# Weights of the first layer ahead of the rows, weight copies on ScalarE, and exactness looks moved between layers, in a graph network on one Trainium2 core

## The chip, the core and the metric

The kernel runs on one core of a Trainium2 chip. The core has a matrix engine (TensorE, PE in the profile; its weight loads are listed apart as PEld), a vector engine (VectorE, DVE), an activation engine (ScalarE, ACT), GpSimd (POOL) and SyncE (SP), which here only issues transfers. SP, ACT and POOL each have their own queue of DMA issues. Each engine works through its own instructions in order; semaphores order them between engines.

The metric is device time in microseconds (us), the median of several runs of one launch.

## The reference

Sixteen graphs of 1024 nodes with 128 features, each with a 1024 by 1024 matrix `adj` of zeros and ones. Two blocks of four layers. The first is a gated network, each graph for itself; the second normalizes over all graphs after each layer. Cut to what matters:

```python
# block 0: h = relu(layernorm(x)), then for i in range(4):
hw = einsum('bnc,cd->bnd', h, weight[i])
m = einsum('bjn,bjd->bnd', adj, hw)
h = gru_cell(m, h, w_ih[i], w_hh[i], b_ih[i], b_hh[i])
x = x + h * mask
# gru_cell: gx = m @ w_ih.T + b_ih; gh = h @ w_hh.T + b_hh
#   r = sigmoid(xr + hr); z = sigmoid(xz + hz); n = tanh(xn + r * hn)
#   h = (1 - z) * n + z * h

# block 1: h = relu(layernorm(x)), then for i in range(4):
h = relu(einsum('bnm,bmc->bnc', adj, h @ W[i]) + b[i])
h = gamma[i] * (h - mean) * rsqrt(var + EPS) + beta[i]   # mean, var over graphs and nodes
x = x + h
```

## The kernel before

The work is in `exact_path`. The features are split into a high part that `fp32r` holds exactly and a low rest; an aggregation with `adj` is a sum of matmuls of both parts with the rows of `adj`. This holds as long as the rows have nothing in their low 16 bits. VectorE looks at each row once for that (`look`, L585 to L589: a maximum over the low halves, 128x1024), and a flag at the end would start a general path, which these inputs don't need.

**Block 0, two streams.** Graphs run in pairs: stream A (`sa`) has the even graphs, stream B (`sb`) the odd ones. `half_step(one, two)` (L823) makes the gates of stream `two` (its matmuls need only h and m) and the aggregation of stream `one`, so that the elementwise work of one hides behind the matmuls of the other. A layer of one graph is: turn h and split it in high (`hw[0]`, ScalarE) and low (`hw[1]`, VectorE), L498 to L503; aggregate with eight rows, 32 matmuls of 512 columns into banks m0 and m1 (L525); copy m from the banks (L750, ScalarE); gates of two halves with six pairs of matmuls each (L762) into four banks g_r, g_hn, g_xn, g_z; sigmoid and tanh on ScalarE (L772 to L778) and five operations on VectorE (L773 to L782). Each gate bank exists once: the second half's matmuls into g_r wait until the first half's sigmoid has read it.

**Weights.** The product `weight[i] @ w_ih[i].T` is made once for each layer. `load_layer` (L457) loads w_hh and w_ih of a layer on SP. `turn_layer` (L466) turns both and weight[i] on TensorE and copies them from the two `tmp` banks; `join_layer` (L484) multiplies and copies w_mT. `load_small` and `turn_small` do the same for biases, gammas and the mask.

**The next pair.** While layer 2 of a stream follows, `ahead` (L787) takes the sums of the next graph's rows of x (`norm_sums`, VectorE), the root (L613, ScalarE, with its own function table), the reciprocal (L617, VectorE) and eight normalizing blocks (L622, ScalarE). `look_on` (L807) makes the looks of a stream's rows: until 3 are done at layer 1, 6 at layer 2 and 8 at layer 3. At layer 1 it also copies and turns the rows for block 1 by GpSimd and SP.

**Order.** For the start (L847 to L952) the order of all five engines is the order of the program, and it is written out by hand: x of graph 0, the rows of `adj` of graphs 0 and 1 (staged as f32, cast by GpSimd or ScalarE in `first_round`), 50 idle transposes for TensorE, norm, split, first aggregation. Weights and looks lie between. After that, only GpSimd and SP keep the program's order; the order of TensorE, VectorE and ScalarE is found by a scheduler when the kernel is built, so that an edit of the looks can move other engines' instructions too.

**Block 1** (L976 to L1149) loads the turned rows again, widens them and aggregates, with the norm over all graphs between layers; then x is added and stored.

Of the kernel before, what the change touches and what calls it, by code (L numbers as in the profile page):

```python
# [8 lines left out]
F32 = mybir.dt.float32  # L9
# [4 lines left out]
AF = mybir.ActivationFunctionType  # L14
ALU = mybir.AluOpType
AX = mybir.AxisListType
P = 128
# [324 lines left out]
def exact_path(  # L342
# [89 lines left out]
    def load_small(prep):  # L432

        vn = prep.tile([P, C], F32, tag="vn", name="vn", bufs=1)[:NV, :]
        r0 = 0
        for src in (g_b_ih, g_b_hh):
            nc.scalar.dma_start(vn[r0 : r0 + 3 * L, :], src.rearrange("l (g c) -> (l g) c", c=C))
            r0 += 3 * L
        for src in (c_b, c_gamma, c_beta):
            nc.scalar.dma_start(vn[r0 : r0 + L, :], src)  # L440
            r0 += L
        mn = prep.tile([P, P], F32, tag="mn", name="mn", bufs=1)
        nc.scalar.dma_start(mn, nodemask.rearrange("b (k p) -> (b k) p", p=P))
        return vn, mn

    def turn_small(vn, mn):
# [19 lines left out]
    def turn_layer(prep, w_g, i):  # L466

        pt = tmp(f"pt_whh{i}")
        for g in range(3):
            nc.tensor.transpose(pt[:, g * P : (g + 1) * P], wns["hh", i][:, g, :], ident)  # L470
        nc.vector.tensor_copy(w_hhT[:, i, :], pt[:, : 3 * P])
        pt = tmp(f"pt_wih{i}")
        for g in range(3):
            nc.tensor.transpose(pt[:, g * P : (g + 1) * P], wns["ih", i][:, g, :], ident)

        w_ihT = prep.tile([P, 3 * C], F32, tag="w_ihT", name=f"w_ihT{i}", bufs=1)
        nc.vector.tensor_copy(w_ihT, pt[:, : 3 * P])
        pg = tmp(f"pt_g{i}")
        nc.tensor.transpose(pg[:, :P], w_g[:, i, :], ident)
        w_gT = prep.tile([P, P], F32, tag="w_gT", name=f"w_gT{i}", bufs=1)  # L480
        nc.vector.tensor_copy(w_gT, pg[:, :P])
        turned[i] = w_gT, w_ihT

    def join_layer(i):  # L484
        w_gT, w_ihT = turned[i]
        pw = tmp(f"pt_wm{i}")
        nc.tensor.matmul(pw[:, : 3 * P], w_gT, w_ihT, start=True, stop=True)
        nc.vector.tensor_copy(w_mT[:, i, :], pw[:, : 3 * P])


    def features_times(w, hT, hw, g, name):
# [42 lines left out]
    with ExitStack() as st:  # L534
# [145 lines left out]
        def behind(*inss):  # L680

            es = ExitStack()
            for ins in () if written[0] else inss:
                es.enter_context(tc.issue_after(ins.ins))
            return es

        class Stream:
# [111 lines left out]
            def finish(self):  # L799

                if self.i == L:
                    self.rest = tail_norm(self.b, self.xt, self.hT)
                    self.b, self.i = self.b + 2, 0
                    if self.b < B:
                        self.take()

            def look_on(self, two):  # L807

                if self.i == 0:
                    return  # L810
                if self.i == 1:
                    if self.b + 2 < B:
                        copy_rows(self.b + 2)
                    adjT = turned_tile(f"adjT{self.b}")
                    for j in range(NB):
                        transpose_rows(self.b, self.rows[j], j, adjT)
                    nc.gpsimd.dma_start(adjT_d[self.b], adjT)
                with behind(two.last_dve):
                    while self.looks < min(3 * self.i, NB):
                        look(self.b, self.rows[self.looks], self.looks)  # L820
                        self.looks += 1

        def half_step(one, two, gated=None, halfway=None):  # L823
# [23 lines left out]
        with tc.tile_pool(name="prep", bufs=1) as prep, tc.manual_schedule(engines=every):  # L847


            pt = tmp("pt_idle")  # L850
            for k in range(50):
                nc.tensor.transpose(pt[:, k % 4 * P : (k % 4 + 1) * P], ident, ident)
            x0 = flat("x0")
            for k0, eng in ((0, nc.sync), (BH, nc.scalar)):
                x0_d = x[0].rearrange("(k p) c -> p k c", p=P)[:, k0 : k0 + BH, :]
                eng.dma_start(x0[:, k0 : k0 + BH, :], x0_d)
            small_in = load_small(prep)
            stage = keep.tile([P, NB, N], BF16, tag="adjT", name="stage", bufs=1).bitcast(F32)
            quarters = [[stage[:, 2 * j : 2 * j + 2, :].rearrange("p a n -> p (a n)")] for j in range(4)]
            late = [[work.tile([P, N], F32, tag="h", name=f"first{j}", bufs=7)] for j in range(4, NB)]  # L860
            raw0 = quarters + late
            first_rows(0, range(4), quarters)
            load_layer(0)
            w_g = flat("w_g")[:, :L, :]
            w_d = g_weight.rearrange("l c d -> c l d")
            nc.sync.dma_start(w_g[:, 0, :], w_d[:, 0, :])
            first_rows(0, range(4, NB), late)
            x1 = load_x(1, nc.sync)
            halves = [[half_tile(f"early{j}_{k}").bitcast(F32) for k in range(2)] for j in range(3)]
            halves.append(  # L870
                [work.tile([P, N], BF16, tag="half1", name=f"early3_{k}", bufs=2).bitcast(F32) for k in range(2)]
            )
            first_rows(1, range(4), halves)
            raw1 = halves + quarters
            h0, h1 = (work.tile([P, N], F32, tag="h", name=f"h_in{b}", bufs=7) for b in range(2))


            sa.open(x0)
            sb.open(x1)
            sa.sums(range(4))  # L880
            norm_root(sa.norm, 0, BH)
            sa.sums(range(4, 5))
            norm_scale(sa.norm, 0, BH)
            sa.sums(range(5, NB))
            sa.normed(range(2))
            norm_root(sa.norm, BH, NB)
            norm_scale(sa.norm, BH, NB)
            sa.normed(range(2, 4))
            sa.split_high(0)
            for j in range(4):  # L890
                sa.rows[j] = first_round(0, j, raw0[j], nc.gpsimd)
            first_look(0, 0, raw0[0])
            sa.split_low(0)
            sa.agg_rows(range(4))
            sa.normed(range(4, NB))
            sa.split_high(1)
            first_look(0, 1, raw0[1])
            sa.split_low(1)
            for j, eng in ((4, nc.scalar), (5, nc.gpsimd)):
                sa.rows[j] = first_round(0, j, raw0[j], eng)  # L900

            turn_small(*small_in)
            turn(sa.y, "in0", h0)
            sa.hT = h0
            first_look(0, 2, raw0[2])
            turn_layer(prep, w_g, 0)
            first_look(0, 3, raw0[3])
            first_rows(1, range(4, NB), quarters)
            sa.agg_rows(range(4, 6))
            join_layer(0)  # L910
            for j, eng in ((6, nc.scalar), (7, nc.gpsimd)):
                sa.rows[j] = first_round(0, j, raw0[j], eng)
            sa.agg_rows(range(6, NB))

            sb.sums(range(NB))
            norm_root(sb.norm, 0, NB)
            norm_scale(sb.norm, 0, NB)
            for j in range(NB):
                sb.rows[j] = first_round(1, j, raw1[j], nc.gpsimd)

            def beside(hf):
                sb.normed(range(hf * BH, (hf + 1) * BH))
                first_look(0, 4 + hf, raw0[4 + hf])

            for hf in range(NH):
                sa.gate_step(hf, lambda: beside(hf))
                sb.split_high(hf)
                sb.split_low(hf)
            for j in (6, 7):
                first_look(0, j, raw0[j])  # L930
            for j in range(4):
                first_look(1, j, raw1[j])
            for i in range(1, L):
                load_layer(i)
            nc.sync.dma_start(w_g[:, 1:, :], w_d[:, 1:, :])
            nc.gpsimd.dma_start(w_c, c_w.rearrange("l c d -> c l d"))
            sb.agg_rows(range(4))
            turn(sb.y, "in1", h1)
            sb.hT = h1
            sb.agg_rows(range(4, NB))  # L940
            sa.ahead()

            def looks():
                for j in range(4, NB):
                    first_look(1, j, raw1[j])

            half_step(sa, sb, looks, lambda: turn_layer(prep, w_g, 1))
            join_layer(1)
            half_step(sb, sa, None, lambda: turn_layer(prep, w_g, 2))
            join_layer(2)  # L950
            turn_layer(prep, w_g, 3)
            join_layer(3)  # L952
# [263 lines left out]
```

## Time and profile before

| | us |
|---|---|
| median of 3 runs | 1866.81 |
| lowest, highest | 1864.57, 1868.89 |
| the profiled execution | 1865.06 |
| its span, first to last instruction | 1863.3 |
| granted TensorE clock, mean | 0.992 |

Busy time of each engine by stage, from the windows view of the profile:

| stage, us | what runs | PE | DVE | ACT | POOL | clock |
|---|---|---|---|---|---|---|
| 0 to 24 | start, first aggregation | 20.46 | 13.55 | 9.43 | 10.02 | 0.93 |
| 24 to 70 | gates and layers 0, 1 of the first pair | 42.14 | 34.70 | 19.44 | 7.91 | 0.96 |
| 70 to 130 | layers 1 to 3 of the first pair | 59.05 | 34.69 | 29.98 | 16.37 | 1.00 |
| 130 to 1233 | the rest of block 0 | 1096.77 | 738.71 | 534.33 | 222.65 | 1.00 |
| 1233 to 1822 | block 1 | 588.65 | 383.00 | 419.85 | 30.71 | 1.00 |
| 1822 to 1863 | last norm, sum, store | 18.73 | 21.94 | 19.33 | 2.62 | 0.74 |

A timeline line has start and duration in us, engine, line of the kernel, operation, what it writes and reads, how many alike are merged (x4), and in brackets the idle time of the engine before it and what ended that. Matmuls overlap, so that the time one takes in the pipeline is longer than the step from one to the next. PEq, ACTq and SPq lines are issues of transfers. Lines of the kernel are given as L and a number.

### The profile page before, as it was taken

What the parts mean: (1) busy time and instruction counts of PE and PEld (TensorE: products, weight loads), DVE (VectorE), ACT (ScalarE), POOL (GpSimd) and SP (SyncE); (2) the same over time, 40 slices, a digit from 0 to 9 for tenths busy, and PEclk for the clock granted to TensorE, in tenths of its full rate; (3) what the DMA queues carried; (4) which work ended last, traced back from release to release, by engine and by line L of the source; (5) the groups of instructions that cost most, each with busy time, mean ns of one, the idle gap of its engine ahead of it and who ended that gap; (6) DMA issues with size and microseconds to landing.
All of it is one profiled execution on the core that took longest, in us unless ns stands there. A gap on an engine that the chain in (4) does not pass through costs nothing. (4 is left out here: it accounts for less than half of the span.)

```text
span 1863.3 us, 21952 instructions
## 1 busy us (share of the span) xinstructions
PE 1825.8 (98%) x7326; PEld 1255.0 (67%) x7326; DVE 1226.6 (66%) x2249; ACT 1032.4 (55%) x1562; POOL 290.3 (16%) x375
## 2 busy tenths in 40 slices
PE   9999999999999999999999999999999999999995
PEld 6556566656656565656665666667778888888884
DVE  7656676666566667667667657676666666666664
ACT  5354453554544445445455453467777768767764
POOL 3042230230131042023023013001100000000021
PEclk9999999999999999999999999999999999999997
DMA  7089776474385376567548546249876666676769
GB/s 253 9 242 300 245 205 226 149 203 165 142 258 181 147 203 192 201 169 223 208 149 203 167 155 175 91 138 333 292 253 227 213 240 222 231 245 209 254 211 258
DMA packets 268433, 381.22 MB, mean 205 GB/s; under 512 B 149812, under 2 KB 171992, under 8 KB 264472
## 3 DMA queue, kind: packets, MB, share of 16 engines
q1 hardware_dynamic: 250112, 245.95, 43.5%
q0 software_dynamic: 17456, 133.45, 20.3%
q8 instruction: 59, 0.97, 0.2%
q14 instruction: 62, 0.51, 0.1%
q10 hardware_dynamic: 744, 0.35, 0.1%
HBM read 287.39 MB, written 117.44 MB: 217 GB/s over the span
## 5 line engine op out<-in xcount | busy, mean ns | idle before, releaser
L525 PE MATMUL pm<-row,ghw 128*128 128x512 f32 x2048 | 520.1, 408 | 2.4 <-ACT ghw L733 1.5
L525 PEld LDWEIGHTS pm<-row,ghw 128*128 128x128 f32 x2048 | 385.0, 189 | 118.8 <-issue 35.9
L525 PE MATMUL pc_m<-wide,chw 128*128 128x512 f32 x1024 | 246.1, 395 | 0.0
L525 PEld LDWEIGHTS pc_m<-wide,chw 128*128 128x128 f32 x1024 | 190.5, 188 | 42.3 <-issue 4.3
L777 ACT ACTIVATE r<-r,vecs 128x512 f32<-128x512 f32 x128 | 92.3, 721 | 215.9 <-DVE r L774 215.8
L525 PE MATMUL pc_g_r<-wide,chw 128*128 128x512 f32 x464 | 187.0, 403 | 0.3 <-ACT chw L502 0.3
L525 PE MATMUL pc_g_z<-wide,chw 128*128 128x512 f32 x464 | 181.0, 390 | 0.0
L594 POOL CAST half<-row 128x1024 bf16<-128x1024 f32 x128 | 140.6, 1114 | 245.9 <-DMA adjT<-half 235.7
L986 DVE CAST wide<-packed 128x1024 fp32r<-128x1024 bf16 x160 | 110.0, 693 | 73.1 <-PE pc_m L525 56.3
L986 DVE CAST wide<-block 128x1024 fp32r<-128x1024 bf16 x160 | 110.2, 691 | 71.9 <-PE pc_g_z L525 36.0
L503 DVE TENSOR_TENSOR ghw<-hw_g,ghw 128x512 fp32r<-128x512 f32 x96 | 62.5, 686 | 121.2 <-ACT ghw L502 121.1
L984 ACT CAST wide<-block 128x1024 fp32r<-128x1024 bf16 x96 | 100.6, 1048 | 60.9 <-PE pc_m L525 34.3
L984 ACT CAST wide<-packed 128x1024 fp32r<-128x1024 bf16 x96 | 100.7, 1049 | 56.5 <-PE pc_g_z L525 27.4
L773 DVE SCALAR_TENSOR_TENSOR r<-g_hn,vecs,r 128x512 f32<-128x512 f32 x128 | 95.3, 744 | 54.4 <-ACT r L772 27.6
L762 PE MATMUL g_xn<-m,w_mT 128*128 128x512 f32 x256 | 130.7, 592 | 0.0
L762 PE MATMUL g_z<-m,w_mT 128*128 128x512 f32 x256 | 130.7, 592 | 0.0
L762 PE MATMUL g_r<-m,w_mT 128*128 128x512 f32 x256 | 130.7, 592 | 0.0
L589 DVE TENSOR_REDUCE low<-row 128x1 f32<-128x1024 uint16 x112 | 130.1, 1204 | 0.0
L750 ACT COPY m<-pm 128x512 f32<-128x512 f32 x128 | 68.6, 587 | 108.6 <-PE pm L525 108.3
L778 ACT ACTIVATE z<-g_z,brz 128x512 f32<-128x512 f32 x128 | 87.2, 681 | 67.7 <-PE g_z L762 67.4
L772 ACT ACTIVATE r<-g_r,brz 128x512 f32<-128x512 f32 x128 | 87.7, 686 | 61.4 <-PE g_r L762 60.3
L1023 DVE BATCH_NORM_STATS2 stats<-feat 128x6 f32<-128x512 f32 x128 | 84.2, 685 | 48.8 <-ACT feat L1022 47.5
(144 smaller groups left out, 2752.9 us busy)
## 6 DMA issues: line engine op xcount, KB each, us to landing
packed<-adjT_d SPq DMA_DIRECT2D x256, 256.0 KB, 6.1
block<-adjT_d SPq DMA_DIRECT2D x256, 256.0 KB, 4.3
raw<-in_adj_dram POOLq DMA_DIRECT2D x112, 512.0 KB, 11.7
row<-raw SPq DMA_DIRECT2D x112, 512.0 KB, 5.4
adjT_d<-adjT POOLq DMA_DIRECT2D x16, 2048.0 KB, 7.8
xmid_d<-x POOLq DMA_DIRECT2D x16, 512.0 KB, 4.6
y<-ymid_d POOLq DMA_DIRECT2D x16, 512.0 KB, 5.2
xo<-xmid_d POOLq DMA_DIRECT2D x32, 256.0 KB, 6.5
```

The costliest lines, as they stand in the source:

```text
L525: nc.tensor.matmul(pm[hf], hw[s][:, j * P : (j + 1) * P], rows[j][:, hf * HALF : (hf + 1) * HALF], start=(j == 0 and s == 0), stop=(j == N ...
L589: nc.vector.tensor_reduce(low[:, k : k + 1], lows, axis=AX.X, op=ALU.max)
L594: nc.gpsimd.tensor_copy(t, row.bitcast(F32))
L750: nc.scalar.copy(m, self.pm[hf])
L762: nc.tensor.matmul(po, wT[:, i, g * C : (g + 1) * C], rhs, start=start, stop=stop)
L772: nc.scalar.activation(r, pr, AF.Sigmoid, bias=brz[:, 3 * i : 3 * i + 1])
L773: nc.vector.scalar_tensor_tensor(r, phn, b_hn(i), r, ALU.add, ALU.mult)
L777: nc.scalar.activation(r, r, AF.Tanh, bias=b_in(i))
L778: self.last_act = nc.scalar.activation(z, pz, AF.Sigmoid, bias=brz[:, 3 * i + 1 : 3 * i + 2])
L984: nc.scalar.copy(r, t)
L986: nc.vector.tensor_copy(r, t)
L1023: nc.vector.bn_stats(stats[:, b * NH + hf, :], dst)
```

## The change

Three edits of the start, and one of the looks.

- The weights of layer 0 (`load_layer(0)` and weight 0) are issued on SP directly behind x's first half, ahead of all rows. Their turn stands ahead of the norm's sums, their join behind the first two normalized blocks. The 50 idle transposes become 20 in front and 30 behind the join. A Sqrt of one column on ScalarE in front of its x transfer loads that table.
- The four copies of `turn_layer` and `join_layer`, for all four layers, go from VectorE to ScalarE.
- The six small transfers go from ScalarE's to GpSimd's queue; in the built order the first of them stands between the two GpSimd instructions that make the identity matrix. `turn_small` moves from ahead of y's turn to behind rows 4 and 5 of the first aggregation.
- `look_on` makes up to four looks at a time, and none when `two` stands at layer 2 with a graph to come, which is when that graph's sums are taken.

```diff
-            nc.scalar.dma_start(vn[r0 : r0 + 3 * L, :], src.rearrange("l (g c) -> (l g) c", c=C))
+            nc.gpsimd.dma_start(vn[r0 : r0 + 3 * L, :], src.rearrange("l (g c) -> (l g) c", c=C))
...
-        nc.vector.tensor_copy(w_hhT[:, i, :], pt[:, : 3 * P])
+        nc.scalar.copy(w_hhT[:, i, :], pt[:, : 3 * P])
...
-        nc.vector.tensor_copy(w_ihT, pt[:, : 3 * P])
+        nc.scalar.copy(w_ihT, pt[:, : 3 * P])
...
-        nc.vector.tensor_copy(w_gT, pg[:, :P])
+        nc.scalar.copy(w_gT, pg[:, :P])
...
-        nc.vector.tensor_copy(w_mT[:, i, :], pw[:, : 3 * P])
+        nc.scalar.copy(w_mT[:, i, :], pw[:, : 3 * P])
...
+                if two.i == 2 and two.b + 2 < B:
+                    return
                 with behind(two.last_dve):
-                    while self.looks < min(3 * self.i, NB):
-                        look(self.b, self.rows[self.looks], self.looks)
+                    for j in range(self.looks, min(self.looks + 4, NB)):
+                        look(self.b, self.rows[j], j)
                         self.looks += 1
...
-            for k in range(50):
-                nc.tensor.transpose(pt[:, k % 4 * P : (k % 4 + 1) * P], ident, ident)
+
+            def idle(n):
+                for k in range(n):
+                    nc.tensor.transpose(pt[:, k % 4 * P : (k % 4 + 1) * P], ident, ident)
+
+            idle(20)
+            root = small.tile([P, 1], F32, tag="root", name="root")
+            nc.scalar.activation(root, eps_t, AF.Sqrt)
...
             small_in = load_small(prep)
+            load_layer(0)
+            w_g = flat("w_g")[:, :L, :]
+            w_d = g_weight.rearrange("l c d -> c l d")
+            nc.sync.dma_start(w_g[:, 0, :], w_d[:, 0, :])
...
-            first_rows(0, range(4), quarters)
-            load_layer(0)
...
-            nc.sync.dma_start(w_g[:, 0, :], w_d[:, 0, :])
-            first_rows(0, range(4, NB), late)
+            first_rows(0, range(NB), raw0)
...
             sb.open(x1)
+            turn_layer(prep, w_g, 0)
             sa.sums(range(4))
...
             sa.normed(range(2))
+            join_layer(0)
+            pt = tmp("pt_idle1")
+            idle(30)
             norm_root(sa.norm, BH, NB)
...
-            turn_small(*small_in)
             turn(sa.y, "in0", h0)
             sa.hT = h0
-            first_look(0, 2, raw0[2])
-            turn_layer(prep, w_g, 0)
-            first_look(0, 3, raw0[3])
+            for j in range(2, 4):
+                first_look(0, j, raw0[j])
             first_rows(1, range(4, NB), quarters)
             sa.agg_rows(range(4, 6))
-            join_layer(0)
+            turn_small(*small_in)
```

More of the change, by code (lines that the diff above doesn't have):

```diff
@@ L436, in load_small @@
         for src in (g_b_ih, g_b_hh):
-            nc.scalar.dma_start(vn[r0 : r0 + 3 * L, :], src.rearrange("l (g c) -> (l g) c", c=C))
+            nc.gpsimd.dma_start(vn[r0 : r0 + 3 * L, :], src.rearrange("l (g c) -> (l g) c", c=C))
             r0 += 3 * L
         for src in (c_b, c_gamma, c_beta):
-            nc.scalar.dma_start(vn[r0 : r0 + L, :], src)
+            nc.gpsimd.dma_start(vn[r0 : r0 + L, :], src)
             r0 += L
         mn = prep.tile([P, P], F32, tag="mn", name="mn", bufs=1)
-        nc.scalar.dma_start(mn, nodemask.rearrange("b (k p) -> (b k) p", p=P))
+        nc.gpsimd.dma_start(mn, nodemask.rearrange("b (k p) -> (b k) p", p=P))
         return vn, mn
@@ L801, in finish @@
                 if self.i == L:
+                    assert self.looks == NB
                     self.rest = tail_norm(self.b, self.xt, self.hT)
@@ L861, in exact_path @@
             raw0 = quarters + late
-            first_rows(0, range(4), quarters)
-            load_layer(0)
-            w_g = flat("w_g")[:, :L, :]
-            w_d = g_weight.rearrange("l c d -> c l d")
-            nc.sync.dma_start(w_g[:, 0, :], w_d[:, 0, :])
-            first_rows(0, range(4, NB), late)
+            first_rows(0, range(NB), raw0)
             x1 = load_x(1, nc.sync)
@@ L898, in exact_path @@
             sa.split_low(1)
-            for j, eng in ((4, nc.scalar), (5, nc.gpsimd)):
-                sa.rows[j] = first_round(0, j, raw0[j], eng)
-            turn_small(*small_in)
+            sa.rows[4] = first_round(0, 4, raw0[4], nc.scalar)
+            sa.rows[5] = first_round(0, 5, raw0[5], nc.gpsimd)
             turn(sa.y, "in0", h0)
             sa.hT = h0
-            first_look(0, 2, raw0[2])
-            turn_layer(prep, w_g, 0)
-            first_look(0, 3, raw0[3])
+            for j in range(2, 4):
+                first_look(0, j, raw0[j])
             first_rows(1, range(4, NB), quarters)
             sa.agg_rows(range(4, 6))
-            join_layer(0)
+            turn_small(*small_in)
             for j, eng in ((6, nc.scalar), (7, nc.gpsimd)):
```

## The prediction

> **What bounds the kernel now.** I read the page first, then busy time by stage, then TensorE's timeline for its idle times, and last the other engines' timelines at each of these.
>
> ```profile
> PE 1825.8 (98%) x7326; PEld 1255.0 (67%) x7326; DVE 1226.6 (66%) x2249; ACT 1032.4 (55%) x1562; POOL 290.3 (16%) x375
> ```
>
> TensorE has work in 98% of the span. Between 1233 and 1822 us it is busy for 588.65 of 589.00 us, and no edit touches that stage or the tail. So the change can win only where TensorE waits, runs at half clock, or does work early that now stands on its path. TensorE's timeline shows these places (start, duration, operation, then the idle time before it and what ended it):
>
> ```profile
> 1.36 7.58 PE L852 MATMUL pt_idle<-ident 128*128 128x128 f32 x50 [1.36 <-POOL ident masks.py:199]
> 10.41 0.70 PE L525 MATMUL pm<-row,ghw 128*128 128x512 f32 x2 [1.47 <-ACT ghw L733]
> 11.42 5.06 PE L525 MATMUL pm<-row,ghw 128*128 128x512 f32 x14 [0.31 <-DVE ghw L737]
> ...
> 62.37 0.33 PE L479 MATMUL pt_g<-ident,w_g 128*128 128x128 f32 x1 [3.10 <-DVE w_hhT L471]
> 62.45 5.50 PE L525 MATMUL pm<-row,ghw 128*128 128x512 f32 x16
> ...
> 93.05 0.91 PE L487 MATMUL pt_wm<-w_ihT,w_gT 128*128 128x384 f32 x2 [0.74 <-DVE w_gT L481]
> ```
>
> Two sets of 16 matmuls take 6.1 and 5.5 us where sixteen take 3.9 at 85.27: the granted clock is 0.71 in 10 to 15 us and 0.83 in 60 to 65. The 3.10 us wait is for a weight copy behind four looks on VectorE:
>
> ```profile
> 57.26 4.59 DVE L589 TENSOR_REDUCE low<-stage 128x1 f32<-128x1024 uint16 x4
> 61.77 0.55 DVE L471 COPY w_hhT<-pt_whh 128x384 f32<-128x384 f32 x1
> ```
>
> In the long stage from 130 to 1233 us TensorE misses 6.2 us in all, in eight waits, of which this is the pattern (VectorE, ScalarE, TensorE):
>
> ```profile
> 239.51 1.18 DVE L589 TENSOR_REDUCE low<-row 128x1 f32<-128x1024 uint16 x1
> ...
> 240.70 2.31 DVE L589 TENSOR_REDUCE low<-row 128x1 f32<-128x1024 uint16 x2
> 242.93 0.19 DVE L617 RECIPROCAL rs_in<-rs_in 128x8 f32<-128x8 f32 x1
> ```
>
> ```profile
> 240.81 0.30 ACT L613 ACTIVATE rs_in<-mv_in,eps_t 128x8 f32<-128x8 f32 x1 [4.31 <-DVE mv_in L610]
> ...
> 243.36 3.18 ACT L622 ACTIVATE y_in<-x,ms_in,rs_in 128x128 f32<-128x128 f32 x8 [0.77 <-DVE ms_in L618]
> ...
> 247.51 1.28 ACT L772 ACT_TABLE_LOAD   x1
> ```
>
> ```profile
> 249.54 1.12 PE L762 MATMUL g_r<-h,w_hhT 128*128 128x512 f32 x2 [0.88 <-ACT r L772]
> ```
>
> Looks delay the last sum and the reciprocal; ScalarE normalizes late, loads the sigmoid's table late, and frees the g_r bank late.
>
> **What the Trainium skill says.** "TensorE: Matmul & The Clock Gate", Part 1: the clock starts at half and is raised after a busy window of about 3.4 us; the windows run freely. The trace agrees: the idle transposes step by 0.213 us until 5.26, then by 0.109; both slow pieces follow a poor window. I use its window below. The same page (Architectural detail) calls ScalarE and VectorE strict FIFO, so an early copy that waits holds everything behind it. "ScalarE: Activation LUTs", What ACT_TABLE_LOAD costs: about 1283 ns a load; here 1.28 us. "DMA: Bandwidth & Descriptors", Queues, rings and completion order: an engine consumes descriptors in ring order; weights put ahead of rows on SP therefore push the rows back. No view isolates that here.
>
> **The change part by part.** The sum is against the profiled execution: 1865.06 us with a span of 1863.3. The median of the three runs is 1866.81, 1.75 above.
>
> *Start, to the first gates (24.00).* Removed from TensorE's path between 16.5 and 24.0: the three turns and the join of layer 0 with their waits. Before, the stretch from the last of the first 16 matmuls (16.41) to the gates takes 7.6 us. What stays: y's turn 0.9, rows 4 and 5 1.9, small vectors 0.5, rows 6 and 7 2.0: 5.3 us.
> Added in front: ident comes 0.9 us later, because a GpSimd DMA now stands between its two parts (such an issue takes 0.89 at 33.00); 20 idle transposes at mostly 0.213 take the engine from 2.25 to about 6.3 (5.9 to 6.5, by where the window falls). The weights (448 KB behind x's first half, sharing the engines with the second, at the 200 to 343 GB/s of the first 10 us, plus 0.6 for landing) are there by about 6.2. Turns to 6.9; ScalarE's three copies 7.0 to 8.3 (0.47 each estimated from 0.587 for 512 columns and 0.39 between 128-column operations); root 8.3 to 8.6 instead of 6.60. The preloaded Sqrt table only makes up for this: before, the root waited for the 1.28 us load. Then scale, two blocks, the join's copy (0.5), second root, two blocks and the high cast: 12.1 instead of 10.27. The join matmul ends at 9.05 and 30 idle transposes at 0.109 end at 12.3. So the first aggregation starts at 12.3, not 10.41; warm, 16 matmuls take 3.7, to 16.1. Rows: some 1.3 us later than before for the first (landed about 7.5, 8.8, 10.1, 11.4), casts on GpSimd 1.04 each, its six issues over by 6.7: not late. The gates start at 21.4: **2.6 us won**. If the window from 5.3 to 8.7, which I put at 70% busy, counts as idle, the 30 transposes run half slow and the start slips 1.5 more: 1.1 won. (45% busy before 12.1 was too little; 78% around 93 was enough.) If the weights land earlier: 3.5.
> This must pass the next chain too: second graph's sums, root, table load, sigmoid (27.71), then VectorE packed from 28.4 to 40.2. Its sums follow the vectors' copies (19.5) and x1's landing (19.95 before, about 18.5 now): sigmoid at 24.7, 3.0 won. So 2.6 holds.
>
> *Layer 1's turn (59 to 68).* ScalarE is idle from 55.7 to 67.8, so the copies follow the turns at once; pt_g starts at 59.5 instead of 62.37 (a bank must still be copied), 2.9 won. No empty window, so no half clock: 16 matmuls in 3.9 instead of 5.5, 1.6 won. The last copy now stands behind two m copies: 0.1 lost. **4.4 won**, 3.5 to 4.8.
>
> *Layers 2 and 3 (83 to 103).* The waits of 0.74 and 0.21 go. But ScalarE now has eight more copies of about 0.5 among eight normalizing blocks (3.2), m copies and two table loads; in the built order w_mT of layer 2 stands behind both m copies, so the gate's m part waits about 1.1. **0**, from 1 won to 1 lost.
>
> *Looks.* Sixteen per pair of graphs as before: A and B each had 3, 3, 2 at layers 1, 2, 3; now A has 4, 0, 4 and B 0, 4, 4. One look is 1.2 us; the additions lie in VectorE's idle times (4.0 us before 300.39, 3.1 before 318.86, against 2.3 more). The built order changes too. At the first place ScalarE now normalizes ahead of the m copies: root 239.65, blocks 240.45 to 243.65, m copies to 244.65, high casts to 245.7, table to 247.0, sigmoid to 247.7. TensorE has moved its m parts behind the h parts, reaches them at 245.0 (the first m copy ends at 244.2), and wants g_r's bank at about 248.1. No wait: six times about 1 us, 5.5 in all, won. At the second (about 268) the build puts 4 instead of 9 matmuls in front of g_r and the blocks ahead of the second m copy: sigmoid ends at 268.4, TensorE arrives at 268.1: 0.35 lost six times, less the 0.63 that two such waits cost today: 1.5 lost. **4.0 won**, 1.5 to 6.
>
> Sum: 2.6 + 4.4 + 0 + 4.0 = 11.0, 1854.1 against the profiled execution, 1855.8 against the median. I take 1855.
>
> **Rivals.** *(a) Head eaten, swaps in the long stage.* The half clock or late weights leave 1 us of the head, layers 2 and 3 lose 1, and the second place takes as much as the first gives: 4.4, 1861. For: idle work now stands in order ahead of real work, and ScalarE is fullest just there (4.53 of 5 us from 90 to 95). Against: 12 us of idle ScalarE at 59 cannot fail to help.
> *(b) All covers hold.* Weights early, no wait at 92, none at 268: 3.5 + 4.8 + 1 + 6 = 15, 1851. For: the estimates at 268 are a third of a microsecond. Against: each must go well.
> *(c) Slower: normalizing in front of the m copies.* ScalarE's place at 241 to 248 becomes the bound. If the reciprocal comes no sooner than today (242.93), the blocks end at 246.5, the m copies at 247.6 and the sigmoid at 250.7: g_r starts 1.2 later than today, six times, 7 lost where I have 5.5 won. The sum is then 2.6 + 4.4 - 7 - 1.5, 1.5 slower: 1867 to 1868, and each further microsecond costs 6 more. It begins to cost when the reciprocal is 0.4 later than my 240.1, and is worse than today from about 1.7. For: the order is fixed when built, whatever the data do. Against: with no look between, the last sum ends at 239.6 on durations from the trace.
> *(d) No change.* GpSimd's issues or the clock spoil the head by 5 us and (a)'s rest holds: about 1865. For: the first 25 us are bound by transfers at 328 GB/s. Against: rows have some 1 us to spare.
>
> **How the numbers follow.** Forecast 0.57 (own range 1851.5 to 1858.5), (a) 0.17, (b) 0.12, (c) 0.06, (d) 0.08. Range 1850.5 to 1862: from (b) to past (a), leaving (c), (d) and a little of (b) out. 0.2% of 1866.8, about what a measurement can tell from no change, is 3.7 us. Faster: forecast, (b) and nearly all of (a): 0.83. Same: (d) and a rest of (a): 0.1. Slower: (c) and a rest of (d): 0.07.
>
> **What would show it.** Head: first aggregation near 12.3 at full clock, first gates near 21.4. Layer 1: no idle time over 0.5 before pt_g, no half clock from 63. Layers 2 and 3: a wait of about 1 us for m or w_mT. Long stage: no wait at the first place, about 0.3 at the second. Wrong if the clock falls during the 30 idle transposes, if the g_r waits stay at 1 us, or if the m part of g_r waits for ScalarE.

## The result, and the profile after

The changed kernel takes 1849.50 us (median of 6 runs, 1848.65 to 1849.94); the kernel before 1865.95 (6 runs, 1864.12 to 1868.89, among them the three of the table of times). The ratio is 0.9911, 95% interval 0.9898 to 0.9923. So it is 16.5 us faster where 11 were forecast, and the time lies 1 us below the range. The profiled spans are 1863.3 and 1847.1 us, 16.2 apart; landmarks on TensorE and ScalarE say where these were won:

| landmark (us from the start of the span) | before | after | won so far | forecast |
|---|---|---|---|---|
| first gate matmul | 24.00 | 22.18 | 1.8 | 2.6 |
| first sigmoid (L772) | 27.71 | 25.68 | 2.0 | 3.0 |
| first split of layer 1 (hw_g) | 43.60 | 41.84 | 1.8 | 2.6 |
| gates behind layer 1's turn | 69.75 | 63.54 | 6.2 | 7.0 |
| hw_g behind layers 2 and 3's turns | 110.14 | 102.72 | 7.4 | 7.0 |
| first sum of the last stage (pc_m) | 1233.67 | 1217.82 | 15.9 | 11.0 |
| end of span | 1863.3 | 1847.1 | 16.2 | 11.0 |

First the page's part 1, busy time by engine:

```profile
PE 1818.7 (98%) x7326; PEld 1253.2 (68%) x7326; DVE 1226.0 (66%) x2233; ACT 1037.1 (56%) x1579; POOL 294.7 (16%) x381
```

The same number of matmul records, 7326, is busy for 7.1 us less than before. A part is the half clock that is gone. The rest is a first hint that time counted as busy before was partly waiting.

TensorE's timeline of the changed kernel in the head (start, duration, operation, idle time before it and what ended that):

```profile
8.51 3.44 PE L857 MATMUL pt_idle<-ident 128*128 128x128 f32 x30
12.27 0.70 PE L525 MATMUL pm<-row,ghw 128*128 128x512 f32 x2 [0.32 <-ACT ghw L733]
13.85 3.48 PE L525 MATMUL pm<-row,ghw 128*128 128x512 f32 x14 [0.88 <-DVE ghw L737]
...
22.18 1.02 PE L762 MATMUL g_r<-h_in,w_hhT 128*128 128x512 f32 x2
```

The first sums start at 12.27 as forecast (12.3), at full clock, but wait 0.88 us for the low part. Layer 1's turn in the same timeline:

```profile
57.72 0.33 PE L479 MATMUL pt_g<-ident,w_g 128*128 128x128 f32 x1 [0.24 <-ACT w_hhT L471]
57.80 3.92 PE L525 MATMUL pm<-row,ghw 128*128 128x512 f32 x16
61.57 0.81 PE L487 MATMUL pt_wm<-w_ihT,w_gT 128*128 128x384 f32 x2
```

The 3.10 us wait is 0.24, and sixteen sums take 3.9 us in place of 5.5.

In the long stage the trace shows no idle time over 0.05 us on TensorE any more. To see what went, look at the first place of the second pair in the kernel before, TensorE and then ScalarE. (In each pair of graphs, the first place is where the next norm of the first stream is made, about 249 us in the first pair; the second, about 268 us, is that of the second stream.)

```profile
397.43 1.02 PE L762 MATMUL g_z<-m,w_mT 128*128 128x512 f32 x2
398.49 1.46 PE L525 MATMUL pm<-row,ghw 128*128 128x512 f32 x4
400.97 1.13 PE L762 MATMUL g_r<-h,w_hhT 128*128 128x512 f32 x2 [1.02 <-ACT r L772]
```

```profile
394.78 3.19 ACT L622 ACTIVATE y_in<-x,ms_in,rs_in 128x128 f32<-128x128 f32 x8 [1.28 <-DVE ms_in L618]
397.88 1.04 ACT L502 CAST ghw<-hw_g 128x512 fp32r<-128x512 f32 x2
398.94 1.28 ACT L772 ACT_TABLE_LOAD   x1
400.23 0.69 ACT L772 ACTIVATE r<-g_r,brz 128x512 f32<-128x512 f32 x1
```

and at the same place of the changed kernel:

```profile
389.06 1.02 PE L762 MATMUL g_z<-m,w_mT 128*128 128x512 f32 x2
389.52 1.03 PE L525 MATMUL pm<-row,ghw 128*128 128x512 f32 x2
390.39 1.02 PE L762 MATMUL g_r<-h,w_hhT 128*128 128x512 f32 x2
```

```profile
382.61 3.19 ACT L622 ACTIVATE y_in<-x,ms_in,rs_in 128x128 f32<-128x128 f32 x8 [0.47 <-DVE ms_in L618]
385.70 1.04 ACT L750 COPY m<-pm 128x512 f32<-128x512 f32 x2
386.65 1.06 ACT L502 CAST ghw<-hw_g 128x512 fp32r<-128x512 f32 x2
387.72 1.28 ACT L772 ACT_TABLE_LOAD   x1
389.02 0.69 ACT L772 ACTIVATE r<-g_r,brz 128x512 f32<-128x512 f32 x1
```

Read it by starts, and by each matmul (a narrow window of the timeline shows them one by one). Before, the last g_z matmul starts at 397.86 and the second sum 0.97 us later, at 398.83; after, at 389.49 and 390.16, 0.67 later. The sums before then step by 0.34 to 0.39 us in place of 0.23: the first two wait for the high cast of 397.88, the next two for the low part behind it (VectorE's subtraction ends at 399.16). Almost none of this is idle time in the trace; the 1.02 us in front of g_r is. And even that is too little: the record of the last sum lasts 0.39 us where the step is 0.23, so the first 0.16 us of a wait behind a sum lie inside the sum's record.

A measure that holds both is the time from the start of the last gate matmul to the start of g_r, summed over the six pairs. The builds put different numbers of sums between, each worth a step of 0.23 us, which is taken off:

| kernel | first place: sums between, us | won against before | second place: sums between, us | won against before |
|---|---|---|---|---|
| before | 4, 16.01 | | 9, 16.02 | |
| changed | 2, 5.71 | 16.01 - 5.71 - 12 x 0.23 = 7.5 | 4, 9.16 | 16.02 - 9.16 - 30 x 0.23 = 0.0 |
| e1, looks alone | 2, 6.10 | 7.1 | 4, 9.16 | 0.0 |
| e5, second stream's looks | 2, 5.97 | 7.3 | 7, 17.08 | -3.8 |
| e6, first stream's looks | 4, 16.23 | -0.2 | 4, 9.15 | 0.0 |

The rows of e1, e5 and e6 are used below. Of the 8.4 us that the changed kernel wins between 110.14 and 1233.67, the first place is 7.5; the other 0.9 I have not attributed. In e1's profile the same stage is 7.1 us shorter, all of it at the first place; in the profiles of e2 and e3, which keep the old looks, it is 0.5 shorter and 0.6 longer than before.

The 0.0 at the second place is a balance of two waits, and not the absence of one. An unhindered TensorE steps by 0.43 us from the last gate matmul and by 0.231 to 0.233 from each sum, so it needs 2.51 with nine sums and 1.36 with four. Before, four of the six pairs take 2.50 to 2.52, the other two 3.02 and 2.96: 0.96 lost. In the changed kernel every pair takes 1.52 to 1.54, as here at the second place of the first pair (TensorE, then ScalarE):

```profile
258.26 1.50 PE L525 MATMUL pm<-row,ghw 128*128 128x512 f32 x4
259.76 1.13 PE L762 MATMUL g_r<-h,w_hhT 128*128 128x512 f32 x2
```

```profile
259.01 0.69 ACT L772 ACTIVATE r<-g_r,brz 128x512 f32<-128x512 f32 x1
```

The fourth sum starts at 259.36 and g_r 0.40 later in place of 0.23: it waits for the sigmoid, which ends at 259.70, 0.05 ahead of g_r, as at the first place above (400.92 and 400.97). So g_r's bank still costs 0.16 us in each pair, 1.0 in all, and the trace shows no idle time for it.

### The profile page after: what moved, and what is told of

The parts are those of the page before. It is cut to its first block, busy times and chain, and to the rows that moved or that the text cites. A ratio compares the mean times of both kernels' runs of the same rounds, so it can differ in the third digit from the quotient of the medians.

```text
span 1847.1 us, 21960 instructions
## 1 busy us (share of the span) xinstructions
PE 1818.7 (98%) x7326; PEld 1253.2 (68%) x7326; DVE 1226.0 (66%) x2233; ACT 1037.1 (56%) x1579; POOL 294.7 (16%) x381
## 5 line engine op out<-in xcount | busy, mean ns | idle before, releaser
L503 DVE TENSOR_TENSOR ghw<-hw_g,ghw 128x512 fp32r<-128x512 f32 x96 | 62.0, 686 | 131.5 <-ACT ghw L502 131.3
L773 DVE SCALAR_TENSOR_TENSOR r<-g_hn,vecs,r 128x512 f32<-128x512 f32 x128 | 95.4, 745 | 58.5 <-ACT r L772 33.1
L589 DVE TENSOR_REDUCE low<-row 128x1 f32<-128x1024 uint16 x112 | 128.5, 1209 | 0.0
L772 ACT ACTIVATE r<-g_r,brz 128x512 f32<-128x512 f32 x128 | 87.7, 685 | 61.6 <-PE g_r L762 60.5
L780 DVE TENSOR_TENSOR h<-h,r 128x512 f32<-128x512 f32 x96 | 77.3, 805 | 62.1 <-ACT r L777 62.1
```

The source lines that it names most:

```text
L589: nc.vector.tensor_reduce(low[:, k : k + 1], lows, axis=AX.X, op=ALU.max)
L772: nc.scalar.activation(r, pr, AF.Sigmoid, bias=brz[:, 3 * i : 3 * i + 1])
L773: nc.vector.scalar_tensor_tensor(r, phn, b_hn(i), r, ALU.add, ALU.mult)
L780: nc.vector.tensor_sub(ho, hin, r)
```

## The experiments

All were timed in five rounds beside the kernel before, on one chip for each group (e1 to e4, e5 to e8, e9 to e12); the kernel before took 1865.98, 1865.01 and 1864.87 us there. The changed kernel's 1849.50 and 0.9911 come from another session. Small differences to it are therefore not settled by the times: for e7 to e12 the difference of the medians and that of the ratios (times 1865 us) lie up to 1.6 us apart. Where they matter, both are given, and the profiles decide.

| kernel | median us | ratio to before, 95% | first gates | first hw_g of layer 1 |
|---|---|---|---|---|
| e1, before + looks | 1857.64 | 0.9956 (0.9942 to 0.9970) | 24.13 | 43.38 |
| e2, changed, old looks | 1858.00 | 0.9958 (0.9944 to 0.9971) | 21.71 | 41.75 |
| e3, before + copies on ScalarE | 1860.24 | 0.9970 (0.9958 to 0.9982) | 24.76 | 43.24 |
| e4, changed + means in PSUM | 1850.06 | 0.9913 (0.9899 to 0.9927) | 22.00 | 41.96 |
| e5, before + second stream's looks | 1860.85 | 0.9979 (0.9972 to 0.9986) | 24.15 | 43.31 |
| e6, before + first stream's looks | 1865.28 | 1.0001 (0.9993 to 1.0010) | 24.15 | 43.38 |
| e7, changed, layers 2, 3 on VectorE | 1850.11 | 0.9923 (0.9909 to 0.9937) | 22.11 | 41.77 |
| e8, changed, no 30 transposes | 1850.80 | 0.9924 (0.9910 to 0.9937) | 24.71 | 43.21 |
| e9, changed, small transfers on ScalarE | 1850.01 | 0.9922 (0.9909 to 0.9936) | 21.30 | 42.03 |
| e10, e4 + lows ahead of looks | 1848.73 | 0.9915 (0.9902 to 0.9929) | 21.67 | 41.45 |
| e11, changed + two casts on ScalarE | 1848.03 | 0.9910 (0.9895 to 0.9925) | 22.10 | 40.61 |
| e12, e10 and e11 | 1848.40 | 0.9911 (0.9896 to 0.9926) | 21.91 | 41.90 |

**The parts alone.** Each of three kernels does one part of the change.

e1, on the kernel before:

```
-    while self.looks < min(3 * self.i, NB):
-        look(self.b, self.rows[self.looks], self.looks)
+    if two.i == 2 and two.b + 2 < B: return
+    for j in range(self.looks, min(self.looks + 4, NB)):
+        look(self.b, self.rows[j], j)
...
```

> The kernel before with the one edit of the looks (4, 0, 4 and 0, 4, 4); start, layer turns and weight copies stay. My theory: the gain of the whole change is a sum of places that do not touch each other, and the long stage's part (8.4 us between the first hw_g after 125 us and 1394 us) comes from the looks alone, because they held the last sums of the coming norm and with them ScalarE's normalizing, both high casts, the table load and the g_r bank. Then this kernel is 8 us faster than before (7.5 to 9), all eight waits of 0.27 to 1.03 us for the g_r bank between 245 and 1026 us are gone, and nothing moves ahead of 125 us. Rival: the long stage's part comes from the order that was built anew once the copies and the start had moved, and the looks alone move the waits about: then 0 to 4 us faster, and waits of 0.3 us or more stay in front of g_r.

Measured: 8.3 faster (7.5 by the two profiles' spans), no idle time over 0.15 us in front of g_r; ahead of 125 us TensorE's landmarks differ by 0.3 us at most. The rival falls. One thing stays joined: with the new looks the build also puts ScalarE's blocks ahead of the m copies and two sums in place of four ahead of g_r at the first place, in e1 and e5 as in the changed kernel. No run has the looks without that order, so how the 7.1 us divide between them is not shown.

e2 is the changed kernel with the first form of these lines.

> The changed kernel with the looks of the kernel before (3, 3, 2 for both graphs); start, turns and ScalarE copies as changed. My theory: 7.4 us faster than before (head 1.8, layer 1's turn 4.4, layers 2 and 3 1.2), within 1 us, and the waits for the g_r bank of 0.9 to 1.0 us stand again at the first place of each pair. Rival (the new order gives the long stage's part): 13 to 16 us faster.

Measured: 8.0 faster, first-place waits of 0.6 to 1.03 us back in all six pairs. 8.3 and 8.0 make 16.3 of the 16.5: as far as these times tell, looks and start do not touch each other.

e3, on the kernel before:

```
-        nc.vector.tensor_copy(w_hhT[:, i, :], pt[:, : 3 * P])
+        nc.scalar.copy(w_hhT[:, i, :], pt[:, : 3 * P])
(the same for w_ihT, w_gT and w_mT)
```

> The kernel before with the four weight copies of each layer on ScalarE in place of VectorE and nothing else; layer 0 is still turned between 16 and 24 us. My theory: layer 1's turn no longer stands behind four looks on VectorE (4.4 us), the copies of layers 2 and 3 no longer hold the next norm's sums (1.2 us), so 5.6 us faster plus what layer 0 does: its copies now share ScalarE with a row cast and two turns' copies, from 1 us won to 1 lost. 4.6 to 6.6 us faster; pt_g of layer 1 without a wait over 0.5 us. Rival: layer 1's 4.4 us came only together with the head (idle ScalarE at 59 us is filled by other work when layer 0 stays): under 3 us.

Measured: 5.7 faster; pt_g of layer 1 waits 0.24 us, and its hw_g landmarks show 0.4 won at 43, 4.4 between 43 and 68, 1.2 between 68 and 110. So two of the three start gains need neither the early weights nor the queue, only the copies' engine.

**Which looks count.** In e5 the new rule holds for the second stream alone, in e6 for the first:

```
+    if self.tag == "B" and two.i == 2 and two.b + 2 < B: return     (e5; "A" in e6)
+    upto = min(self.looks + 4, NB) if self.tag == "B" else min(3 * self.i, NB)
-    while self.looks < min(3 * self.i, NB):
+    while self.looks < upto:
...
```

(In e6 the second line has "A" too.)

> The kernel before with the new looks for the second stream alone (0, 4, 4), which frees the first place of each pair, where the first stream's norm is made (about 249 us); the first stream keeps 3, 3, 2. My theory, from the steps of TensorE between the last gate matmul and the next g_r: the first place cost 16.0 us in six pairs where an unhindered TensorE takes 8.1, so about 7.6 us of the looks' 8.3 lie here, part of them hidden in busy records of the four sums ahead of g_r. Expected: 7 to 8 us faster than before. Rival, as my forecast had it: only the idle time that the trace shows in front of g_r is there to be won, 5.5 us.

> The kernel before with the new looks for the first stream alone (4, 0, 4), which frees the second place of each pair (about 268 us), where the second stream's norm is made; the second stream keeps 3, 3, 2. My theory: nothing to win and nothing lost, 0 to 1 us faster than before; the waits of 0.9 to 1.0 us at the first place stay. Rival, the forecast's term: 1.5 us slower, with waits of about 0.3 us in front of g_r at the second place.

Measured: e5 wins 4.2 (its 17 runs spread from 1858.69 to 1864.71), e6 nothing. Both of my figures for e5 fail: the first place is freed in full (7.3 in the table above), and the second takes 3.8 of it back. VectorE and then ScalarE of e5 at the second place of the second pair:

```profile
409.77 1.18 DVE L589 TENSOR_REDUCE low<-row 128x1 f32<-128x1024 uint16 x1
410.87 0.17 DVE L610 BATCH_NORM_AGGREGATE mv_in<-st_in 128x2 f32<-128x6 f32 x1
410.96 2.31 DVE L589 TENSOR_REDUCE low<-row 128x1 f32<-128x1024 uint16 x2
413.19 0.19 DVE L617 RECIPROCAL rs_in<-rs_in 128x8 f32<-128x8 f32 x1
```

```profile
413.75 3.18 ACT L622 ACTIVATE y_in<-x,ms_in,rs_in 128x128 f32<-128x128 f32 x8 [0.92 <-DVE ms_in L618]
416.84 0.56 ACT L502 CAST ghw<-hw_g 128x512 fp32r<-128x512 f32 x1
417.42 1.28 ACT L772 ACT_TABLE_LOAD   x1
418.71 0.69 ACT L772 ACTIVATE r<-g_r,brz 128x512 f32<-128x512 f32 x1
```

It is the first place's chain again, look for look. VectorE and ScalarE have the same order at this place in the kernel before, where the sigmoid ends at 420.67 and g_r starts at 420.73, right on its step of 0.23. There TensorE, held up at the first place and with nine sums ahead of g_r, comes to the second late enough for the chain to cost little; once the first is free, it costs. That is why e6 alone is worth nothing, and the second stream's norm has to be freed too for 8.3.

**Layers 2 and 3.** In e7 the four copies are `(nc.scalar.copy if i < 2 else nc.vector.tensor_copy)(...)`.

> The changed kernel with the weight copies of layers 2 and 3 back on VectorE; layers 0 and 1 stay on ScalarE. My theory: these copies stood between 83 and 103 us ahead of VectorE's sums of the next norm, and moving them to ScalarE won 1.2 us in place of the 0 that I forecast: 1.0 to 1.5 us slower than the changed kernel, with waits of 0.2 to 0.7 us in front of the join and the first hw_g in that stretch. Rival: the 1.2 us came with the earlier start of the stage, and it makes no difference (within 0.4 us).

Measured: waits of 0.74 and 0.21 us back at 86.76 and 88.33, and from the split of layer 1 to the hw_g behind these turns 62.08 us in place of 60.88: 1.2 lost. The time is 0.6 above the changed kernel's by medians, 2.2 by ratios: in the right direction, but not told from nothing by the timing. The layers' 1.2 rests on the profiles of e3 and e7.

**The clock.** e8 leaves `idle(30)` out; it is warming work and no part of the result.

> The changed kernel without the 30 idle transposes after the join of layer 0; the 20 ahead of it stay. They keep TensorE busy from 9 to 12.3 us. Theory: without them the granted clock is at half when the first 16 matmuls start, these take up to 3 us more in part of the stretch from 12 to 17 us, and the first gates come 1 to 1.6 us later than 22.18: 0.8 to 1.6 us slower than the changed kernel. Rival: rows and weights bind the stretch (row 7 lands at 17.4), so that half clock costs nothing there: within 0.4 us.

Measured: the granted clock is 0.53 between 12 and 17 us where the changed kernel has 1.00, the gates come 2.5 us later (24.71), yet the split of layer 1 only 1.4 (43.21), and the time 1.3 by medians, 2.4 by ratios. The rival falls, but more than a microsecond of delay vanishes between 25 and 43 us. Where it goes is seen below: VectorE's operations L781 and L782, which take 1.34 and 1.41 us in the changed kernel, come at 32.42 and 33.15 here, behind GpSimd's last cast (over at 30.92), and take 0.69 each.

**The head, and what binds behind it.** e4, on the changed kernel:

```
+    if self.b == 0:
+        self.norm[1] = acc("g_xn", "mv_psum")[:, : 2 * NB].rearrange("p (k w) -> p k w", w=2)
```

> The changed kernel with the means and variances of the first graph's first norm in a PSUM bank that is free until the gates, in place of SBUF; nothing else. In the changed kernel the two small products of mean and root (128x4, 0.17 us elsewhere) took 1.02 and 1.03 us, each beside one of GpSimd's row casts and ending with it. My theory: an operation of VectorE with both inputs in SBUF waits for the whole cast of GpSimd; with one of them in PSUM it does not. Then both take 0.2 us or less beside the cast, the first aggregation starts 0.7 to 0.9 us earlier than 12.27, the first gates 0.5 to 0.9 earlier than 22.18, and the whole is 0.5 to 1 us faster than the changed kernel. Rival 1: the product waited for its own input (the reciprocal's result) or for an access that any operation suffers beside a cast: it still takes about 1 us. Rival 2: it is short but rows 0 to 3 bind: gates at 22.2 as before.

Measured: the products (L618) take 0.16 us, inside casts of GpSimd at 9.23 and 10.76. Rival 1 falls. But the weights came late in this execution (w_ih at 7.89 us, 6.14 in the changed kernel's), so the sums start at 13.23, without a wait. The gates come 0.2 earlier and the time doesn't fall: what the shorter products are worth in time is open.

e10 is e4 with `split_low` ahead of `first_look` twice; e9 is the changed kernel with the six transfers of `load_small` on `nc.scalar`.

> The changed kernel with the first norm's means in PSUM and, on VectorE, both low parts of the first split ahead of the looks at rows 0 and 1 that stood before them. Theory: the 0.88 us that the sums of the changed kernel wait for the low part (13.85), and with it the 0.8 us of the head that my forecast had and the chip did not give, are VectorE's: the products held by GpSimd's casts and the look ahead of the low part. First gates at 21.0 to 21.6 if the weights land by 6.7, and the whole time 0.5 to 1 us under the changed kernel. Rival: what follows is bound elsewhere, by VectorE's chain from 26 to 38 us: gates at 21 to 22, but the first sums of the second graph's second half stay within 0.3 us of 38.5, and the time within 0.4 us.

> The changed kernel with the six small transfers (biases, vectors, node mask) back on ScalarE's queue. Theory: what binds the head of the changed kernel is when the weights and rows land and how VectorE gets through; the six issues of 0.5 to 0.7 us on GpSimd only delay ident to 2.43, which the wait for the weights at 5.4 to 6.7 hides. Then the time is within 0.5 us of the changed kernel, ident is there at 1.4 and the first aggregation stays at 12 to 12.7. Rival: on ScalarE's queue the issues share the way with the weights' issues, the weights land 1 us or more later, and the first gates slip behind 22.7.

Measured: the gates come at 21.67 and 21.30, what I had forecast for the change itself (21.4), but the split of layer 1 at 41.45 and 42.03 against 41.84: earlier gates buy 0.4 us and -0.2. (In e10 the two low parts, now ahead of the looks, meet casts of GpSimd themselves and take 1.5 us each.) In e9 ident is there at 1.37 and the time above the changed kernel's, by 0.5 or 2.1, so the small transfers' queue is worth nothing that shows. What the split goes with is the landing of row 7 of the second graph: in the changed kernel, e2, e4, e7, e9 and e10 that row lands at 30.25 to 30.93 and the split comes 11.1 to 11.5 us later each time, wherever between 21.3 and 22.2 the gates start. The link is VectorE between 26 and 38 us. Its timeline in the changed kernel, and GpSimd's casts beside it:

```profile
28.99 0.68 DVE L780 TENSOR_TENSOR h<-h_in,r 128x512 f32<-128x512 f32 x1
29.78 1.34 DVE L781 TENSOR_TENSOR h<-h,z 128x512 f32<-128x512 f32 x1
31.15 1.41 DVE L782 TENSOR_TENSOR h<-h,r 128x512 f32<-128x512 f32 x1
32.48 0.68 DVE L737 TENSOR_TENSOR ghw<-y_in,ghw 128x512 fp32r<-128x512 f32 x1
```

```profile
29.36 2.65 POOL L565 CAST row<-stage 128x1024 fp32r<-128x1024 f32 x2 [0.26 <-DMA stage<-in_adj_dram]
```

L781 and L782 take twice their usual 0.69 beside the casts of rows 6 and 7. The casts follow the rows' landing (29.31 and 30.66), so an earlier start of VectorE's chain only makes more of it meet casts. e11 takes these two off GpSimd (and its loop of GpSimd casts ends with row 5):

```
+    if hf == 1: sb.rows[7] = first_round(1, 7, raw1[7], nc.scalar)     (after sb.normed, in beside)
+    if hf == 0: sb.rows[6] = first_round(1, 6, raw1[6], nc.scalar)     (after sb.split_high)
```

> The changed kernel with the casts of rows 6 and 7 of the second graph on ScalarE in place of GpSimd. In the changed kernel two of VectorE's operations with both inputs in SBUF took 1.34 and 1.41 us beside these two casts, where 0.69 is usual, and VectorE has no other idle time over 0.15 us from 27 to 38.4. Theory: that chain of VectorE sets what follows, so the second sums of the second graph start 1.0 to 1.4 us earlier than 38.52 and the whole is 0.8 to 1.4 us faster than the changed kernel. Rival: ScalarE's two casts (1.05 us each) delay its sigmoid, blocks and tanh as much: within 0.4 us.

VectorE in e11:

```profile
29.70 0.69 DVE L781 TENSOR_TENSOR h<-h,z 128x512 f32<-128x512 f32 x1
30.43 0.69 DVE L782 TENSOR_TENSOR h<-h,r 128x512 f32<-128x512 f32 x1
31.04 0.68 DVE L737 TENSOR_TENSOR ghw<-y_in,ghw 128x512 fp32r<-128x512 f32 x1
```

Measured: both 0.69, the split of layer 1 1.2 us earlier and only 10.3 behind row 7's landing (30.29), the first sum of the last stage 1.4 earlier (1216.42): the chain is shown as what binds this stretch. The time is 1848.03 us (4 runs of 1847.21 to 1848.67), the lowest median here and 1.5 under the changed kernel's, but by ratios 0.9910 against 0.9911. That e11 beats the changed kernel rests on the profile; the timing doesn't show it.

> The changed kernel with both: means in PSUM and lows ahead of looks in the first graph's head, and rows 6 and 7 of the second graph cast on ScalarE. Theory: with VectorE's chain freed the earlier gates count as well: 1.3 to 2.3 us faster than the changed kernel, the second sums of the second graph at 36.5 to 37.3. Rival: rows of the second graph (landing until 30.7) bind the stretch, and it is no better than rows 6 and 7 on ScalarE alone.

Measured: 1848.40, no better than e11 alone. The weights landed late again (w_ih at 7.66), the sums started at 13.0, and the second graph's rows landed 1.5 us later than in the changed kernel (row 7 at 32.19). The rival holds for this execution; what both are worth with early weights is open.

## Why the prediction was wrong in size

**Wrong: the looks, "4.0 won".** This is the failed term, and its size is what failed: 8.4 in the changed kernel's profile, 7.1 in e1's, 8.3 by e1's time. Both of its parts were too low.

*"Six times about 1 us, 5.5"* at the first place measured 7.5. I added up the idle time in front of g_r (5.5) and took the four sums ahead of it as work. Against the unhindered 1.36 us of a pair, the place cost 16.0 - 8.2 = 7.8: to the 5.5 come six times 0.16 that the last sum's record covers, and 1.3 in which sums were held by the same late ScalarE chain. The mechanism was the one I named, down to ScalarE's order (blocks, m copies, casts, table, sigmoid); the measure of its price was wrong.

*"0.35 lost six times"*, less 0.63, at the second place came out as 0.0 in place of 1.5 lost. The wait that I forecast is there, of 0.16 us in place of 0.35: 1.0 lost. The two waits of the kernel before cost 0.96 and not 0.63, for the same reason as at the first place. That the two cancel is chance. And what this place costs when only the first is freed, 3.8 more in e5, I had not looked for.

**Wrong by less: the head, 2.6.** First sums as forecast. Two things were missed. The second product of mean and root took 1.03 us beside a cast of GpSimd, and a look of 1.21 stood behind it, so the first low part is done at 13.80 and the sums wait 0.88; in e2, with the same start, that product began just ahead of a cast (11.40 and 11.42), took 0.16, and the gates came at 21.71. And even gates at 21.3 to 21.7 bring little more (e9, e10, e2): the sentence "so 2.6 holds" followed the next chain only up to the sigmoid at 24.7, and the chain behind it is where the gain goes. 1.8 was won.

**Wrong by less: layers 2 and 3, "0".** Measured 1.2. I put ScalarE's eight blocks where they lay before, so that w_mT stood behind them. But VectorE's weight copies had also stood ahead of the norm's sums: the sums start at 85.75 before, 4.0 us after VectorE's last operation of the gates (81.76), and 0.6 us after it in the changed kernel (76.16 and 75.55). ScalarE is through with the blocks in time, and TensorE's m part starts at 85.49 with no wait.

**Right:** layer 1's turn, 4.4 as forecast, both its wait and its half clock; the 30 transposes that keep the clock (e8); the weights, forecast for 6.2 and landing at 6.14 and 6.67 in the changed kernel's profile, though not in every execution; the later ident, which costs nothing that shows (e9). Rival (b), "all covers hold", was nearest with 1851, in part by luck: it had 1.7 us too much in the head and some 2 too little in the looks, and its "none at 268" is not so.

## What to carry to other kernels

Price a wait by the step from start to start against an unhindered neighbour of the same kind, not by idle time: a matmul's record can contain a wait (2.3 of 7.8 us at the first place, all of the 1.0 at the second). Where one chain occurs at two places, free both, or the second takes back part of what the first gave (7.3 won, 3.8 returned in e5). And follow a gain in the head past the next consumer, up to the point where a transfer or another engine fixes the time.

## What was not expected of the hardware

VectorE's operations with both inputs in SBUF are stretched when they start beside a cast of GpSimd; others are not. Mean durations over the changed kernel's profile:

| VectorE operation | inputs | clear of casts | beside a cast (longest) |
|---|---|---|---|
| L781, L782 | SBUF, SBUF | 0.69 | 1.13, 1.25 (2.85) |
| L618, 128x4 | SBUF, SBUF | none here; 0.16 in e9 | 1.02 (1.03) |
| L773, L774 | PSUM, SBUF | 0.74, 0.69 | 0.75, 0.69 (0.75) |
| L503 | PSUM, SBUF | 0.69 | 0.69 (0.69) |
| L589, look | SBUF | 1.21 | 1.21 (1.21) |

The Trainium skill states it, in "SBUF — State Buffer", SBUF: two separate sides: the pair of ports that both engines share is an exclusive lock, held for the whole instruction, and an operation of VectorE with two SBUF inputs takes part in it. The trace agrees: the two products of L618 end at 9.17 and 11.98, with the casts beside them (9.15 and 11.97). e4 shows the way round: with one input in PSUM, 0.16 us beside a cast. The casts pay too: four in a row in e9, beside such operations, took 1.49 to 1.55 us, 1.04 alone.

When weights land differs between executions of nearly the same start: w_ih at 6.14, 6.32, 7.66 and 7.89 us in the changed kernel, e2, e12 and e4, with the issues at the same times within 0.01 us; in e7, e8, e10 and e11 it was 5.93 to 6.01. A head that is bound by them cannot be judged to a microsecond by one profile.
